# Attention in two levels of seven-product blocks: the last batch computes product 6 in whole blocks, and batch 6 puts its fourth pair of scores into product 2's banks

## The chip, the cores and the metric

The kernel runs on one core of one Trainium2 chip. The metric is device time in microseconds (us), the median of the runs. All data is 32-bit floating point. Engines by their short names: PE (TensorE, matrix products), PEld (its weight loads), DVE (VectorE), ACT (ScalarE), POOL (GpSimd) and SP (which only issues transfers).

## The reference

For each of 8 batches, with x of 512 x 1024 and a context x2 of 512 x 1024:

```python
q = einsum('bcn,dc->bnd', x1, Wq) + bq        # 1024 x 64
k = einsum('bcn,dc->bdn', x2, Wk) + bk[:, None]
v = einsum('bcn,dc->bdn', x2, Wv) + bv[:, None]
attn = softmax(einsum('bnd,bdm->bnm', q, k), axis=2)
out = einsum('bcm,bnm->bcn', v, attn) + x1     # 512 x 1024
```

## The kernel before

**The algebra.** Since each row of the attention sums to one, the values are applied last: with e the exponentials of the scores (m by n), y = x2 e, divided by the sums of e over m (the denominators), and out = Wv y + bv + x1. Both products, y and out ("o"), are done in 2 x 2 blocks by seven products instead of eight, as in Strassen's scheme in Winograd's form. The left blocks are called `a` (of x2) or `w` (of Wv), the right blocks `t` (of e) or `y`. `MULT` gives for each product its two operands, its PSUM banks and whether it opens them: 1 is 11 x 11 in banks a; 2 is 12 x 21 in c; 6 is S2 x T2, on a; 7 is S3 x T3, in c; 5 is S1 x T1, on a; 3 is S4 x 22, on a; 4 is 22 x T4, on c. S1 to S4 and T1 to T4 are sums of blocks, made by DVE, by ACT with accumulating transfers, or by transfers alone.

**Whole blocks and a second level.** A product of y can be done in whole blocks (`multiply`, L392: two halves of four matmuls of 128 x 128 by 128 x 512, L407, each half then copied out by ACT, L418), or by a second level of seven inner products of quarter size (L474: two matmuls of 256 columns each, recorded as four). The second level needs sums of its own, made on DVE: four left ones (`inner_left`, L447, 128 x 256 each) and three right ones (`inner_right`, L463 of 128 x 1024, L466 and L467 of 128 x 512). `multiply_seeded` (products 1, 2, 7 and 3) starts in fresh banks and ends with `complete` on DVE (L517). `multiply_joined` (5 and 6) leaves its parts in an SBUF tile d (ACT, L483), completes it (L551) and joins it with banks a (L566, two halves); after product 6, `reseed` (L573) copies the joined sums back into banks a. Their two extra accumulators, "chain" and "third", are taken from the pool `ps_s`, tag "sc", which has two buffers.

**Scores.** `scores_and(n, 0, i_bank, "c", ...)` computes the four pairs of scores of the next batch's first half (L240), each copied by ACT (L249). They use the same two "sc" buffers in turn, but the pair number `i_bank` uses banks c0 and c1 (two copies, L247). Then DVE takes the running maximum (`folds`, L260).

**Order.** The whole order is written out by hand under a manual schedule. `period(s, n, nn, nnn)` is one batch s with the next ones n, nn, nnn (None past the end); each engine executes its own instructions strictly in that order. `weave` interleaves lists of steps, one of each list in turn. The flag `six` says whether product 6 is done in the second level; before the change that holds for batches 2 to 5 and for batch 7, the last one. Batch 6 (where nn is None) does it in whole blocks, and so do 0 and 1.

**The last batch before the change**, in order: product 1; the sums of e for the second denominator (L260) with product 6's sums between them; `total` (L268 on DVE, then POOL's reduction across partitions, L288, and a small transfer, L290); product 2, with hooks on ACT that copy banks a (L361); y11 (L597); the first reciprocal (L296); `begin_s4` and `end_s4`; product 6, with hooks on ACT that copy the first operand of T4 (L349; POOL adds T2 by transfer, L350); the sums for 5 and for 7's left side; completion and joins of 6; reseed; T3 on DVE (L331); 7's right sums; S4's left sums for product 3; product 5, its completion, the second reciprocal, its joins woven with product 3's right sums; product 7 and y22; product 4's sums; product 3; the scaling of y (L588) and its sums (L375, L377); product 4; the scaling of y21; then the seven products of o (1, 6, 2, 5, 7, 4, 3; L427 and L407) and the output (L626, L636, L644, L648).

**S4** of a batch is begun by a load on SP's queue (L167) and finished by a transfer on POOL's queue that accumulates S2 onto it (L171). In the last batch SP's queue holds, ahead of that load, the last outputs of batch 6 (L664) and the four loads of x1 (L140) that the output adds.

Of the kernel before, what the change touches and what calls it, by code (L numbers as in the profile page):

```python
# [12 lines left out]
ALU = mybir.AluOpType  # L13
# [3 lines left out]
def kernel(  # L17
# [236 lines left out]
    def fold(s, h, i, kind, op):  # L254

        e = s.e[h]
        if i == 1:
            s.mx[h] = sb.tile([P, 2, H], F32, tag="fold", name=f"{kind}_{s.b}_{h}", bufs=2)
        f = s.mx[h]
        nc.vector.tensor_tensor(f, e[:, :, 0, :] if i == 1 else f, e[:, :, i, :], op)  # L260
# [9 lines left out]
    def folds(s, h, kind, op):  # L270

        return [lambda i=i: fold(s, h, i, kind, op) for i in range(1, MH)]

    def weave(*rows):

        for steps in zip_longest(*rows):
            for step in steps:
                if step:
                    step()
# [83 lines left out]
    def sums_e(s, *ks):  # L363
        parts = [{n: v[:, i : i + 2, :] for n, v in s.t.items()} for i in (0, 2)]
        return [lambda k=k, part=part: right_sums(part, k) for k in ks for part in parts]

    def sum_e(s, *ks):
        weave(sums_e(s, *ks))
# [70 lines left out]
    def inner_left(s, i, x, tag):  # L439

        v = {f"{p + 1}{q + 1}": x[:, ts(q, MH // 2), ts(p, P)] for p in range(2) for q in range(2)}
        sums = sb.tile([P, 4, MH // 2, P], F32, tag=tag, name=f"aI{i}_{s.b}")
        v |= {step[0]: sums[:, z] for z, step in enumerate(LEFT)}
        s.inner[i] = v

        def make(k, x, y, op):
            return lambda: nc.vector.tensor_tensor(v[k], v[x], v[y], op)  # L447

        return [make(*step) for step in LEFT]

    def inner_right(s, i, x, *tags):

        v = {
            f"{q + 1}{r + 1}": x[:, ts(q, MH // 2), ts(r, H // 2)] for q in range(2) for r in range(2)
        }
        last = 4 // len(tags)
        shape = [P, last, MH // 2, H // 2]
        sums = [sb.tile(shape, F32, tag=t, name=f"eI{i}{t}_{s.b}") for t in tags]
        both, t2, t4 = sums[0][:, 0:2], sums[-1][:, last - 2], sums[-1][:, last - 1]
        part = x.rearrange("p (q k) (r n) -> p q k r n", q=2, r=2)  # L460
        s.inner[i, "t"] = v | {"T1": both[:, 0], "T3": both[:, 1], "T2": t2, "T4": t4}
        return [
            lambda: nc.vector.tensor_tensor(  # L463
                both, part[:, :, :, 1, :], part[:, 0].rearrange("p k r n -> p r k n"), ALU.subtract
            ),
            lambda: nc.vector.tensor_tensor(t2, both[:, 0], v["22"], ALU.subtract),  # L466
            lambda: nc.vector.tensor_tensor(t4, v["21"], t2, ALU.add),  # L467
        ]
# [101 lines left out]
    def reseed(s):  # L570

        for j in range(2):
            nc.scalar.copy(s.bank["a", j], s.tmp[6][:, j, :])  # L573
# [27 lines left out]
    def evict_y(s, k):  # L601

        weave(evictions_y(s, k))
# [198 lines left out]
    def scores_and(n, h, i_bank, bank, project):  # L802

        for i in range(MH):
            scores(n, h, i, bank if i == i_bank else None)()
        return project()
# [4 lines left out]
    def period(s, n, nn, nnn):  # L811

        late = s.b >= 1
        six = late and (n is None or s.b >= 2 and nn is not None)

        def first(i):
            multiply(s, "y", i, s.a, s.t, MH)
# [17 lines left out]
                load_x(nnn, x1)  # L835

        def scores_0():
            then = scores_and(n, 0, 1, "c", next_queries if nn else nothing)
            if six:
                reseed(s)  # L840
            return then
# [11 lines left out]
        if s.b == 0:  # L853
            open_t(s)
            first(1)
            head_second(s, n)
            sum_e(s, "T1", "T2")
            total(s, 0)
            load_a(n, "11")
            first(2)  # L860
            evict_y(s, "11")
            keys(n)
            load_x(nn, x1)
            sum_t4(s)
            sums(s, 1)
            shares(s, 0)
            sum_e(s, "T3")
            load_a(n, "21", "22")
            first(6)
            scores_0()  # L870
            weave(folds(n, 0, "max", ALU.max))
            fold_halves(n, 0, ALU.max)
            highest(n, 0)
            weave(inner_left(s, 4, s.a["22"], "a12"), inner_right(s, 4, s.t["T4"], "eT2"))
            lefts_3 = inner_left(s, 3, s.a["S4"], "aI3")
            shares(s, 1)
            first(5)
            weave(lefts_3, inner_right(s, 3, s.t["22"], "eT1"))
            for i in range(MH):
                lower(n, 0, i)  # L880
            first(7)
            copy_7(s, 0)
            copy_7(s, 1)
            complete_3 = multiply_seeded(s, 3, "r")
            complete_3()
            evict_t3(s)
            evict_y(s, "22")
            scale_y(s, "T3", "11", "22")
        else:
            complete_1 = multiply_seeded(s, 1, "y11")  # L890
            adds = folds(s, 1, "sum", ALU.add)
            if six:
                weave(
                    adds,
                    [nothing, complete_1] + inner_right(s, 6, s.t["T2"], "yT1", "yT2"),
                    [nothing, nothing] + inner_left(s, 6, s.a["S2"], "i2"),
                )
            else:
                weave(adds, [nothing, complete_1] + inner_left(s, 7, s.a["S3"], "yT4"))
            total(s, 1)  # L900
            hooks = {5: lambda: copy_u1(s, 0), 4: lambda: copy_u1(s, 1)}
            if n:
                hooks |= {6: lambda: sum_t3(s, 0), 3: lambda: sum_t3(s, 2)}
            complete_2 = multiply_seeded(s, 2, "y22", hooks)
            complete_2()
            evict_y(s, "11")
            invert(s, 0)
            begin_s4(s)
            end_s4(s)
            sum_t4(s)  # L910
            evict_q = None
            if six:
                hooks = {6: lambda: copy_t4(s, 0), 5: lambda: copy_t4(s, 2)}
                complete_6, *join_6 = multiply_joined(s, 6, "v", hooks)
                lefts_5 = [] if n else inner_left(s, 5, s.a["S1"], "a11")
                weave(
                    inner_right(s, 5, s.t["T1"], "y21", "u1"), lefts_5, inner_left(s, 7, s.a["S3"], "yT4")
                )
                complete_6()
                weave(join_6)  # L920
                if n:
                    evict_q = scores_0()
                    weave(inner_left(s, 5, s.a["S1"], "i2"))
                    weave(folds(n, 0, "max", ALU.max))
                else:
                    reseed(s)
                    sum_e(s, "T3")
            else:
                copy_t4(s, 0)
                copy_t4(s, 2)  # L930
                first(6)
                weave(inner_right(s, 5, s.t["T1"], "y21", "u1"), inner_left(s, 5, s.a["S1"], "i2"))
                evict_q = scores_0()
                weave(folds(n, 0, "max", ALU.max))
            rights_7 = inner_right(s, 7, s.t["T3"], "yT1", "yT2")
            weave(rights_7, [nothing, nothing] + inner_left(s, 3, s.a["S4"], "aI3"))
            complete_5, *join_5 = multiply_joined(s, 5, "r", {6: evict_q} if nn else {})
            complete_5()
            if n:
                fold_halves(n, 0, ALU.max)  # L940
                highest(n, 0)
            spread(s, 0)
            shares(s, 1)
            weave(join_5, inner_right(s, 3, s.t["22"], "eT1"))
            if n:
                lower(n, 0, 0)
            complete_7 = multiply_seeded(s, 7, "y12")
            complete_7()
            evict_y(s, "22")
            if n:  # L950
                for i in range(1, MH):
                    lower(n, 0, i)
            else:
                weave(inner_left(s, 4, s.a["22"], "a12"), inner_right(s, 4, s.t["T4"], "eT2"))

            hooks = {2: lambda: copy_7(s, 0), 5: lambda: copy_7(s, 1)}
            if n:
                hooks |= {6: lambda: exponential(n, 0, 0), 4: lambda: exponential(n, 0, 1)}
            complete_3 = multiply_seeded(s, 3, "r", hooks)
            complete_3()  # L960
            evict_t3(s)
# [153 lines left out]
```

## Time and profile before

| what | us |
|---|---|
| median of 3 runs (lowest, highest) | 685.46 (685.11, 685.80) |
| the profiled execution's own time | 684.92 |
| its span | 683.1 |
| PE busy | 669.0 (98%) |
| DVE busy | 625.4 (92%) |
| ACT busy | 345.8 (51%) |
| POOL busy | 217.7 (32%) |

The span is the time between the first and the last instruction of the profiled execution; its own time, which the runs also measure, is 1.8 us longer. Times within the span are counted from its start. In the windows of the trace the last stages look so:

| stretch | us | PE busy | DVE busy | granted clock |
|---|---|---|---|---|
| 579.4 to 603.4: products of o, batch 6 | 24.00 | 24.00 | 23.76 | 1.00 |
| 603.4 to 615.4: products 1 and 2, batch 7 | 12.00 | 12.00 | 11.30 | 1.00 |
| 615.4 to 630.9: product 6 and the start of 5 | 15.50 | 8.42 | 15.47 | 1.00 |
| 630.9 to 655.2: the rest of 5, then 7, 3 and 4 | 24.30 | 24.30 | 21.65 | 0.93 |
| 655.2 to 683.1: products of o, output | 27.90 | 24.10 | 15.25 | 0.98 |

A busy time of PE is not PE at its peak, and the share over the whole span is an average over stages with different limits. The mean granted clock of the execution is 0.997.

### The profile page before, as it was taken

The numbers are of one execution on the slowest core, as the hardware profiler recorded it, in microseconds if no ns is written. First come the engines' busy times: TensorE is split into PE (matmuls) and PEld (weight loads), VectorE is DVE, ScalarE is ACT, GpSimd is POOL, SyncE is SP. The second block draws the span as 40 slices with busy tenths as digits, with TensorE's granted clock in tenths as the row PEclk, the third lists the DMA queues.
The fourth block names the chain that finished last, engine by engine and source line by source line (L and its number), as shares of the span: only waits on it lengthen the run. The fifth ranks groups of instructions, "written<-read, shape, count | busy, mean of one in ns | idle before, by whom it ended". The sixth has DMA issues, their size and how long they took to land.

```text
span 683.1 us, 7499 instructions
## 1 busy us (share of the span) xinstructions
PE 669.0 (98%) x2504; PEld 415.0 (61%) x2504; DVE 625.4 (92%) x826; ACT 345.8 (51%) x595; POOL 217.7 (32%) x189
## 2 busy tenths in 40 slices
PE   9999999999999999999999999999999999995997
PEld 5333554756558665668647685486755676474863
DVE  1999998989999999999999999999999889999884
ACT  2734266546455564473754656545645548443320
POOL 0124215341435314451144512434143621443100
PEclk9999999999999999999999999999999999999999
DMA  9666658997996969969699796998789784498503
GB/s 302 267 204 228 153 214 146 253 192 229 249 246 186 228 181 292 227 183 262 172 277 237 162 284 171 257 249 155 233 197 192 222 174 73 93 207 264 120 14 110
DMA packets 52790, 138.45 MB, mean 203 GB/s; under 512 B 5776, under 2 KB 8080, under 8 KB 52752
## 3 DMA queue, kind: packets, MB, share of 16 engines
q0 software_dynamic: 23472, 58.27, 47.3%
q1 hardware_dynamic: 28992, 79.31, 32.0%
q10 hardware_dynamic: 288, 0.39, 0.2%
q8 instruction: 20, 0.33, 0.2%
q14 instruction: 18, 0.15, 0.1%
HBM read 90.97 MB, written 16.81 MB: 158 GB/s over the span
## 4 chain that ended last, share of the span: by engine, by line
PE 93%; DVE 4%; DMA 1%; ACT 1%; issue 1%; SPq 0%; DVEq 0%; ACTq 0%
PE ps_oa L407 12%; PE ps_ya L474 10%; PE ps_oc L407 8%; PE ps_yc L474 8%; PE ps_s L240 6%; PE ps_ya L407 5%; PE ps_o L407 4%; PE ps_o L427 4%; PE ps_q L193 4%; PE ps_k L193 3%; PE ps_i4chain L474 3%; PE ps_i3chain L474 3%; PE ps_i5chain L474 3%; PE ps_i7chain L474 3%; PE ps_i1chain L474 3%; PE ps_i2chain L474 2%
## 5 line engine op out<-in xcount | busy, mean ns | idle before, releaser
L288 POOL PARTITION_ALL_REDUCE den<-half x16 | 51.6, 3225 | 91.2 <-DVE half L268 91.2
L283 POOL PARTITION_ALL_REDUCE top<-max x16 | 31.7, 1980 | 131.3 <-DVE few L296 58.2
L318 DVE TENSOR_TENSOR e<-e,top 128x1024 f32<-128x1024 f32 x60 | 69.8, 1213 | 0.0
L322 ACT ACTIVATE e<-e 128x1024 f32<-128x1024 f32 x60 | 61.8, 1057 | 6.2 <-DVE e L318 5.5
L407 PE MATMUL ps_oa<-yT,w_S 128*128 128x512 f32 x128 | 57.5, 592 | 0.0
L407 PE MATMUL ps_oc<-yT,w 128*128 128x512 f32 x128 | 57.4, 592 | 0.0
L667 POOL DMA_DIRECT2D sum<-e x21 | 28.9, 1377 | 84.3 <-ACT sum L672 36.1
L249 ACT COPY e<-ps_s 128x1024 f32<-128x1024 f32 x46 | 45.6, 1031 | 12.2 <-PE ps_s L240 7.2
L240 PE MATMUL ps_s<-q,k 64*128 64x512 f32 x188 | 47.8, 608 | 0.9 <-ACT q L693 0.8
L407 PEld LDWEIGHTS ps_oa<-yT,w_S 128*128 128x128 f32 x128 | 24.3, 190 | 30.6 <-issue 30.6
L407 PEld LDWEIGHTS ps_oc<-yT,w 128*128 128x128 f32 x128 | 24.3, 190 | 30.6 <-issue 29.9
L260 DVE TENSOR_TENSOR max<-max,e 128x1024 f32<-128x1024 f32 x30 | 36.7, 1222 | 2.2 <-DVE max L260 0.5
L418 ACT COPY uo<-ps_oa 128x512 f32<-128x512 f32 x32 | 18.7, 585 | 35.1 <-PE ps_oa L407 34.0
L240 PEld LDWEIGHTS ps_s<-q,k 64*128 64x128 f32 x188 | 17.0, 186 | 23.0 <-issue 16.3
L511 ACT COPY ps_ya<-ps_i1chain 128x256 f32<-128x256 f32 x28 | 10.0, 357 | 40.8 <-PE ps_i1chain L474 37.3
L588 DVE TENSOR_TENSOR y<-y,den 128x1024 f32<-128x1024 f32 x24 | 30.4, 1293 | 0.3
L407 PE MATMUL ps_oa<-y,w_S 128*128 128x512 f32 (+1 forms) x68 | 28.8, 567 | 0.0
L407 PE MATMUL ps_o<-y,w 128*128 128x512 f32 x64 | 28.8, 592 | 0.0
L427 PE MATMUL ps_o<-y,w 128*128 128x512 f32 x64 | 28.8, 592 | 0.0
L407 PE MATMUL ps_ya<-eT,aS 128*128 128x512 f32 x64 | 28.3, 595 | 0.0
L193 PE MATMUL ps_k<-x_in_x_dram,wqk_sb 128*64 128x512 f32 x112 | 26.0, 600 | 0.4 <-DMA x_in_x_dram<-in_x_dram 0.4
L331 DVE TENSOR_TENSOR eT<-eT,e 128x1024 f32<-128x1024 f32 x16 | 26.1, 1637 | 0.0
(217 smaller groups left out, 1655.1 us busy)
## 6 DMA issues: line engine op xcount, KB each, us to landing
x_in_x_dram<-in_x_dram SPq DMA_DIRECT2D x60, 512.0 KB, 8.4
a<-in_x2T_dram SPq DMA_DIRECT2D x32, 512.0 KB, 9.9
sum<-e POOLq DMA_DIRECT2D x21, 512.0 KB, 9.1
aS<-in_x2T_dram SPq DMA_DIRECT2D x14, 512.0 KB, 6.3
aS<-in_x2T_dram POOLq DMA_DIRECT2D x14, 512.0 KB, 7.6
uo<-in_x_dram POOLq DMA_DIRECT2D x14, 512.0 KB, 10.4
r<-in_x_dram POOLq DMA_DIRECT2D x14, 512.0 KB, 11.2
out_dram<-r SPq DMA_DIRECT2D x14, 512.0 KB, 4.6
```

The lines of the kernel that those rows point to most:

```text
L193: nc.tensor.matmul(ps[r, :], w_sb[:, c, :], s.x[:, c, ts(h, H)], start=(c == 0), stop=(c == CT - 1),)
L240: nc.tensor.matmul(ps[g], s.k[r, ts(i, P)], s.q[r, ts(h, H)], start=True, stop=True)
L249: nc.scalar.copy(e[:, :, i, :], whole)
L260: nc.vector.tensor_tensor(f, e[:, :, 0, :] if i == 1 else f, e[:, :, i, :], op)
L283: nc.gpsimd.partition_all_reduce(s.top[h], s.half[h], P, ReduceOp.max)
L288: nc.gpsimd.partition_all_reduce(s.den[h], s.half[h], P, ReduceOp.add)
L318: nc.vector.tensor_tensor(e, e, top, ALU.subtract)
L322: nc.scalar.activation(e, e, AF.Exp)
L407: nc.tensor.matmul(ps[:, n], left[ka][:, k, ts(j, P)], right[kb][:, k, n], start=opens and k == 0, stop=i in (2, 3, 4) and k == n_k - 1, s ...
L427: nc.tensor.matmul(ps, w["11"][:, k, ts(j, P)], s.y["11"][:, k, :], start=k == 0, stop=False, skip_group_check=True)
L474: nc.tensor.matmul(ps, s.inner[i][ka][:, k, :], s.inner[i, "t"][kb][:, k, :], start=opens and k == 0, stop=z in (2, 3, 4) and k == MH // 2 ...
L588: nc.vector.tensor_tensor(s.y[k], s.y[k], rden, ALU.mult)
```

## The change

Two things change in `period`. The flag `six` no longer holds for the last batch: its product 6 is done in whole blocks, so its inner sums, completion, joins and the reseeding copies are no longer there, and the copies of T4 stand before the product. Product 7's four left sums in the last batch move from beside product 5's sums to behind T3, beside 7's right sums. And in batch 6 (where nn is None) the pair of scores that uses banks c is number 3, the fourth, instead of number 1, the second.

```diff
-        six = late and (n is None or s.b >= 2 and nn is not None)
+        six = s.b >= 2 and nn is not None
...
-            then = scores_and(n, 0, 1, "c", next_queries if nn else nothing)
+            then = scores_and(n, 0, 1 if nn else 3, "c", next_queries if nn else nothing)
...
+            elif n:
+                weave(adds, [nothing, complete_1] + inner_left(s, 7, s.a["S3"], "yT4"))
             else:
-                weave(adds, [nothing, complete_1] + inner_left(s, 7, s.a["S3"], "yT4"))
+                weave(adds, [nothing, complete_1])
...
             if six:
                 hooks = {6: lambda: copy_t4(s, 0), 5: lambda: copy_t4(s, 2)}
                 complete_6, *join_6 = multiply_joined(s, 6, "v", hooks)
-                lefts_5 = [] if n else inner_left(s, 5, s.a["S1"], "a11")
                 weave(
-                    inner_right(s, 5, s.t["T1"], "y21", "u1"), lefts_5, inner_left(s, 7, s.a["S3"], "yT4")
+                    inner_right(s, 5, s.t["T1"], "y21", "u1"), [], inner_left(s, 7, s.a["S3"], "yT4")
                 )
                 complete_6()
                 weave(join_6)
-                if n:
-                    evict_q = scores_0()
-                    weave(inner_left(s, 5, s.a["S1"], "i2"))
-                    weave(folds(n, 0, "max", ALU.max))
-                else:
-                    reseed(s)
-                    sum_e(s, "T3")
+                evict_q = scores_0()
+                weave(inner_left(s, 5, s.a["S1"], "i2"))
+                weave(folds(n, 0, "max", ALU.max))
             else:
                 copy_t4(s, 0)
                 copy_t4(s, 2)
                 first(6)
                 weave(inner_right(s, 5, s.t["T1"], "y21", "u1"), inner_left(s, 5, s.a["S1"], "i2"))
-                evict_q = scores_0()
-                weave(folds(n, 0, "max", ALU.max))
+                if n:
+                    evict_q = scores_0()
+                    weave(folds(n, 0, "max", ALU.max))
+                else:
+                    sum_e(s, "T3")
             rights_7 = inner_right(s, 7, s.t["T3"], "yT1", "yT2")
+            if n is None:
+                weave(rights_7, inner_left(s, 7, s.a["S3"], "yT4"))
+                rights_7 = []
             weave(rights_7, [nothing, nothing] + inner_left(s, 3, s.a["S4"], "aI3"))
```

For batches 0 to 5 the instructions and their order are the same as before.

## The prediction

> **What bounds the kernel now.** I read the page first, then the chain of waits over the last two batches, then each engine's timeline there.
>
> ```profile
> span 683.1 us, 7499 instructions
> ...
> PE 93%; DVE 4%; DMA 1%; ACT 1%; issue 1%; SPq 0%; DVEq 0%; ACTq 0%
> ```
>
> TensorE (PE) carries 93% of the chain, so in most of the span work taken from another engine buys nothing. The last batch is the exception. The chain of waits shows VectorE (DVE) alone ending last from 608.69 to 629.3 (start us, length us, what):
>
> ```profile
> 613.36 1.23 DVE sum L260
> ...
> 616.32 1.14 DVE eI6yT L463
> ...
> 626.68 1.34 DVE aI L447 x4
> ...
> 628.63 0.61 DVE d L566
> ...
> 629.32 0.66 ACT ps_ya L573 x2
> ...
> 630.86 2.07 PE ps_i5chain L474 x4
> 632.93 1.60 PE ps_ya L474 x4
> ```
>
> The sums for product 6 (L463 to L467, L447), the sums for 5 and 7, the completion of 6 and its joins (L551, L566) and the two reseeding copies stand between PE and product 5. PE's timeline shows what they cost it there: idle 1.54 us before 617.93, 0.77 before 619.81 and 4.77 before 630.86, 7.1 us in all. Behind the last of them it also runs at half clock (the windows; the column after POOL is the granted clock):
>
> ```profile
> 628.00:630.90 2.90, 0.04 (x1) 0.04 (x1) 2.90 (x6) 1.58 (x4) 0.72 (x2) 1.00 0.24 89
> 630.90:632.00 1.10, 1.10 (x3) 0.92 (x4) 1.10 (x2) 0.18 (x1) 1.10 (x4) 0.50 0.44 82
> ...
> 635.00:636.00 1.00, 1.00 (x6) 0.88 (x5) 0.82 (x3) 0.57 (x2) 0.00 (x0) 1.00 1.14 221
> ```
>
> Two cold groups of four records there took 2.07 and 1.60 us where a warm one takes 0.86: 1.95 us more.
>
> The next limit is a transfer, not an engine. Product 3 of this batch needs S4, which is loaded on SP's queue behind the four loads of x1, and completed by an accumulating transfer from POOL's queue:
>
> ```profile
> 618.08 2.92 SPq L140 DMA_DIRECT2D x_in_x_dram<-in_x_dram  x4
> 621.12 0.55 SPq L167 DMA_DIRECT2D aS<-in_x2T_dram  x1
> ```
>
> ```profile
> 630.18 0.88 POOL L171 DMA_DIRECT2D aS<-aS  x1 [4.70 <-DMA aS<-in_x2T_dram]
> ```
>
> ```profile
> 635.15 0.76 DVE L447 TENSOR_TENSOR aI<-aS 128x256 f32<-128x256 f32 x2 [0.35 <-DMA aS<-aS]
> ...
> 642.73 0.70 DVE L517 TENSOR_TENSOR ps_yc<-ps_yc,v 128x512 f32<-128x512 f32 x1 [1.58 <-ACT ps_yc L511]
> ...
> 648.77 0.70 DVE L517 TENSOR_TENSOR ps_ya<-ps_ya,v 128x512 f32<-128x512 f32 x1 [0.48 <-ACT ps_ya L511]
> ...
> 659.86 1.22 DVE L588 TENSOR_TENSOR y<-y,den 128x1024 f32<-128x1024 f32 x1
> ```
>
> POOL waited 4.70 us for the load, and the accumulated S4 landed at 635.1: DVE's L447 at 635.15 is the first to read it and waited 0.35 us for it. The other three DVE rows are its waits after that (1.58 for product 7's copies, 0.48 for product 3's) and the scaling of y21, the last thing the third output product waits for.
>
> **The change, part by part.** All times are of this profiled execution: span 683.1, its own time 684.92, which is 0.54 below the median of the three timed runs, 685.46.
>
> Last batch, what goes from DVE. Four left and three right sums for product 6 lie between 616.23 and 620.04: 3.81 us. Completion and joins of 6 lie between 627.95 and 629.75: 1.80 us. Together 5.61 us; the two L573 copies (0.66 in the chain) go from ACT.
>
> What it adds on PE. Whole blocks are eight matmuls of 512 columns; batch 6 does the same and its chain piece "PE ps_ya L407 x16" is 6.87 us. The seven inner products are 7 x 0.86 = 6.04. So 0.83 us more PE work, but it waits for no sums: T2 is ready at 612.1, the copies of the bank at 615.8, so product 6 runs 615.37 to 622.24. On ACT two 0.58 us evictions of u6 replace six small copies.
>
> What moves. Product 7's four left sums (4 x 0.34 us) go from early DVE slots to behind T3 beside product 7's right sums: same work, no transfer of theirs. The copies of T4 on ACT come at about 615.8 instead of 621.21 and 623.20; their two transfers stay behind the S4 accumulation in POOL's queue, so T4 lands as before (by 641). POOL's reduction of the second denominator starts 3.81 us earlier; its small transfer and the row of the first denominator do too, but the second reciprocal stays behind S4 on DVE.
>
> DVE up to S4. The order becomes: sums, total, completion of 2, y11, then product 5's right sums at about 618.7 and its lefts by 622.8, T3 by 625.1, product 7's sums by about 629. Product 5 can start at 622.24, needs its first sums at 623.1 (ready 620.6), and ends at 628.3; product 7 follows from 628.3 to 634.3, its sums always ready first. So the three PE stalls (7.1) and the cold clock (1.95) go: 9.05 - 0.83 = 8.2 us by that. PE's product 7 ends at 634.3 where it ended at 643.17, 8.9 earlier (the rest are the waits of some tenths between them).
>
> What is late next: S4. DVE now reaches S4's left sums at 634.80 - 5.61 = 629.2 and waits there until 635.15; nothing in the change touches SP's queue, where S4 stands behind the x1 loads, and the accumulation is issued by POOL only when that load is in. Queued behind that wait on DVE are product 5's completion and joins, product 3's right sums, product 7's completion, y22 and product 4's sums. PE waits for it too, in product 3. So 5.6 of the 5.61 us saved turn into a wait, and from 635.15 on DVE runs as before, less the waits that a product 7 finished 8.9 us earlier takes away: 1.58 before 642.73 and 0.48 before 648.77. That is 2.06 us: y21's scaling ends at 661.08 - 2.06 = 659.02.
>
> PE after S4: product 3's first group 635.2 to 636.06, then a wait for its right sums (eI3, done 639.15), its end 644.9; product 4 to 650.9; two output products of 3.43 to 657.8; then it waits for y21 until 659.05. In the trace of before that third output product started at 661.96, with y21 ready 0.9 us earlier. Gain 661.96 - 659.05 = 2.9 us. From there to the end PE runs through, as before. Both denominators are in by then: the second one's spread is issued at 642.18 and took 3.4 us, needed at 648.6.
>
> Bounds on S4's landing, the one cost that the trace does not fix: if POOL issues quicker beside an idle DVE (L171 took 0.88, the quickest issue in these rows 0.54), 0.3 to 0.5 us better; if transfers collide otherwise, about 1 us worse. I take no change, since queue, source and neighbours are the same.
>
> The clock, a term to weigh. In the trace PE lost its clock after an idle 4.77 us, and not in 615.4 to 620.75, where it stood still 1.54 and 0.77 us. The change leaves 0.9 us idle before 635.2 and 3.1 before 639.15, with 0.86 of work between: between those two rows. Full clock costs 0; half clock 1.95 us on PE, against the 1.3 us that PE waits for y21: 0.65 net. I take 0, nearer to the interrupted idling.
>
> The Trainium skill ("TensorE: Matmul & The Clock Gate", What's actually happening) has the clock fall after one idle window of about 3.4 us; its closing table says to avoid gaps over about 3 us. By the first the 3.1 us gap is safe and the sum stays; by the second it is not and the gain is 2.25. The row of 0.50 after 4.77 us agrees with both, so no run here decides.
>
> Batch 6, the pair of scores in banks c moved from second to fourth. The timelines of ACT and then PE, before:
>
> ```profile
> 547.97 1.08 ACT L247 COPY e<-ps_sc 128x512 f32<-128x512 f32 x2
> 548.92 1.96 ACT L249 COPY e<-ps_s 128x1024 f32<-128x1024 f32 x2
> ```
>
> ```profile
> 550.02 1.13 PE L474 MATMUL ps_i5chain<-eT,aS 128*128 128x256 f32 x4 [0.50 <-ACT e L249]
> ```
>
> Product 5's two banks are freed by the copies of the last two scores in the ordinary banks. They were the third and fourth, so PE started at 550.02 and its second group waited until 551.15. Now they are the second and third: first group at about 549.9, second at 550.75, then a short wait for ACT, which copies the fourth pair first: product 5 ends about 0.4 us earlier on PE. But DVE decides here: its maxima start at 549.09 and run without a gap to 607.45, and the second score, now one copy instead of two, is there within 0.1 us of that. POOL's accumulations at 594 to 603, which feed SP's queue and so S4, come behind DVE's work too. I count 0; ends: 0.4 gained if PE's lead passes through, 0.1 lost if the third score's copy (ready at 550.3) makes DVE wait.
>
> Sum: 2.9 + 0. Span 680.2, profiled execution 682.0, median 685.46 - 2.9 = 682.6 us.
>
> **The rivals.** *S4 does not bind* (its landing follows the rest forward): PE keeps its 8.9 us and DVE follows, median about 676.6. For it: nothing but the size of the stall removed. Against it: 621.12 on SP, behind x1. Chance 0.06.
>
> *The clock falls* in product 3: gain 2.25, median 683.2. Chance 0.17.
>
> *Slower: S4's accumulation takes as long as elsewhere.* In the trace it lands 4.9 us after its issue in the last batch, and 8.6 to 9.5 us in the others that I looked up, where two more accumulations stand ahead of it in POOL's queue. Each us passes straight to DVE's end: +3.7 gives -2.9 + 3.7 = +0.8, median 686.3; +4.6 gives 687.2. It decides, that is, it makes the kernel slower, from about 4.3 us on. Against it: no transfer is put ahead of it. Chance 0.05.
>
> *No difference*: y21's chain is held by something else, such as the T4 transfers landing 2 us later, which then delay product 4's sums by what was won. T4 landed before 641.4 and is now needed at about 643.3 instead of 644.87: 1.9 us of margin. Chance 0.06.
>
> **How the numbers follow.** The forecast has 0.66. What a measurement of this kernel can tell from no change is about 0.2%, 1.4 us, so faster means under 684.1. Forecast, clock and free S4 are all faster: 0.89; no difference and part of the last rivals 0.07; slower 0.04. The range runs from 681.3 (S4 0.5 earlier, 0.4 from batch 6, and some of the free S4 case) to 684.0 (clock 0.65 and S4 0.8 later); outside it are most of the free S4 case and the two bad ones, under 0.2.
>
> **What would show it.** Right: PE's product 6 as L407 on ps_ya without a stall and product 5 and 7 behind it at clock 1.0; DVE idle about 6 us before L447 on aS, released by the transfer aS; about 3 us of PE wait for eI3; the third output product released by DVE's L588. Wrong: S4's L171 transfer landing at another place than 635 us, PE windows of 0.50 in product 3, an idle DVE before product 4's right sums, or DVE's first maximum in batch 6 more than 0.3 us away from 549.1.

## The result and the profile after

The changed kernel's median is 683.23 us (680.67 to 683.57, 9 runs), that of before 685.11 us in the runs beside it; the ratio is 0.9965, with an interval of 0.9954 to 0.9975. That is 2.4 us less (1.7 to 3.2). The profiled executions differ by 684.92 - 682.89 = 2.03 us, and this difference is explained below step by step. The page:

```profile
span 681.1 us, 7459 instructions
...
PE 84%; DMA 8%; DVE 2%; issue 2%; SPq 1%; ACT 1%; POOL 1%; DVEq 0%; POOLq 0%; ACTq 0%
```

DVE's share of the chain is down from 4% to 2%, and transfers, 1% before, are now 8%. Only 14.3 us of that, 2% of the span, are S4's two transfers. The rest lies far ahead, since the chain is now followed back by another way (22.5 us of the kernel's first loads, two accumulating transfers of 5.27 and 11.84 us that end before 608), and says nothing of the last batch. PE's timeline of the last batch (start us, length, engine, line, what, and idle time before it with its releaser):

```profile
615.63 7.03 PE L407 MATMUL ps_ya<-eT,aS 128*128 128x512 f32 x16
...
628.54 1.03 PE L474 MATMUL ps_i7chain<-e,a 128*128 128x256 f32 x4
...
635.86 1.13 PE L474 MATMUL ps_i3chain<-e,aS 128*128 128x256 f32 x4 [1.11 <-DMA aS<-aS]
640.06 1.53 PE L474 MATMUL ps_i3third<-eI3eT,aI 128*128 128x256 f32 x4 [3.07 <-DVE eI3eT L463]
...
659.92 3.60 PE L407 MATMUL ps_o<-y,w 128*128 128x512 f32 x8
```

Product 6 runs in 6.87 us of whole blocks without a wait, 5 follows it and 7 starts at 628.54, where before the change product 5's third group had waited until 630.86. Then PE waits 1.11 us for S4 and 3.07 us for DVE's sums, and its next groups are slow. DVE in the same stretch:

```profile
635.84 0.76 DVE L447 TENSOR_TENSOR aI<-aS 128x256 f32<-128x256 f32 x2 [6.71 <-DMA aS<-aS]
...
641.76 0.69 DVE L517 TENSOR_TENSOR ps_yc<-ps_yc,v 128x512 f32<-128x512 f32 x1
...
647.24 0.69 DVE L517 TENSOR_TENSOR ps_ya<-ps_ya,v 128x512 f32<-128x512 f32 x1
...
658.33 1.23 DVE L588 TENSOR_TENSOR y<-y,den 128x1024 f32<-128x1024 f32 x1
```

DVE waits 6.71 us for S4, where it had waited 0.35. Its former waits of 1.58 and 0.48 us (L517) are gone. Y21 is scaled at 659.56 (658.33 + 1.23), 0.4 us ahead of the product that needs it. The chain that ended last goes through the transfers (start us, length us, what):

```profile
620.94 9.37 DMA aS<-in_x2T_dram
...
630.89 4.92 DMA aS<-aS
...
640.06 1.53 PE ps_i3third L474 x4
641.59 1.71 PE ps_i3chain L474 x4
643.31 1.27 PE ps_ya L474 x4
```

Load of S4, accumulation of S4, then DVE, then PE: that is the order in which the last batch is now held. The windows show why the PE groups from 640.06 on are slow (the third number from the right is the granted clock):

```profile
640.00:641.00 1.00, 0.94 (x4) 0.79 (x4) 1.00 (x2) 0.00 (x0) 0.00 (x0) 0.80 0.92 209
641.00:642.00 1.00, 1.00 (x4) 0.68 (x3) 0.97 (x3) 0.32 (x1) 0.00 (x0) 0.50 0.36 137
...
644.00:645.00 1.00, 1.00 (x6) 0.90 (x5) 1.00 (x1) 0.20 (x1) 0.00 (x0) 1.00 0.61 172
```

### The profile page after: what moved, and what is told of

Read it like the earlier page. It is cut to its first block, busy times and chain, and to the rows that moved or that the text cites. A ratio compares the mean times of both kernels' runs of the same rounds, so it can differ in the third digit from the quotient of the medians.

```text
span 681.1 us, 7459 instructions
## 1 busy us (share of the span) xinstructions
PE 669.5 (98%) x2492; PEld 412.7 (61%) x2492; DVE 620.0 (91%) x816; ACT 344.4 (51%) x590; POOL 218.7 (32%) x189
## 4 chain that ended last, share of the span: by engine, by line
PE 84%; DMA 8%; DVE 2%; issue 2%; SPq 1%; ACT 1%; POOL 1%; DVEq 0%; POOLq 0%; ACTq 0%
PE ps_oa L407 11%; PE ps_ya L474 9%; PE ps_yc L474 7%; PE ps_oc L407 7%; PE ps_s L240 6%; PE ps_ya L407 5%; PE ps_q L193 4%; PE ps_o L407 4%; PE ps_o L427 4%; PE ps_k L193 3%; PE ps_i3chain L474 3%; PE ps_i4chain L474 3%; DMA sum<-e 3%; PE ps_i5chain L474 2%; PE ps_i1chain L474 2%; PE ps_i7chain L474 2%
## 5 line engine op out<-in xcount | busy, mean ns | idle before, releaser
L407 PE MATMUL ps_ya<-eT,aS 128*128 128x512 f32 x80 | 35.4, 595 | 0.0
L588 DVE TENSOR_TENSOR y<-y,den 128x1024 f32<-128x1024 f32 x24 | 30.4, 1294 | 0.3
L303 POOL DMA_DIRECT2D den<-row x16 | 10.0, 624 | 51.3 <-DMA row<-few 51.3
```

The costliest lines, as they stand in the source:

```text
L407: nc.tensor.matmul(ps[:, n], left[ka][:, k, ts(j, P)], right[kb][:, k, n], start=opens and k == 0, stop=i in (2, 3, 4) and k == n_k - 1, s ...
L588: nc.vector.tensor_tensor(s.y[k], s.y[k], rden, ALU.mult)
```

## The experiments

Two theories stand against each other. Mine: all is won in the last batch; S4's landing decides, and from its first reading on DVE, with some tenths from PE's clock. Against it: the moved pair of scores has a share; or S4's wait is incidental, and the scaling of y21 or PE's own work holds the end. Every ratio is to the kernel before, timed beside the kernel in question.

**Only the last batch, and only the pair.** The first kernel changes only the last batch and keeps batch 6's pair in second place; the second is the kernel before with only the pair moved to fourth place. The first against the changed kernel:

```diff
-            then = scores_and(n, 0, 1 if nn else 3, "c", next_queries if nn else nothing)
+            then = scores_and(n, 0, 1, "c", next_queries if nn else nothing)
```

> Only the last batch is changed; batch 6 keeps its second pair of scores in product 2's banks. My theory (all of the gain is made in the last batch, and is bound by the landing of S4): the same as the changed kernel within 0.3 us, that is 0.9965 of before, about 2 us less. Rival (the moved pair gives or takes a part): 0.4 us or more away from the changed kernel, and batch 6's first maximum on DVE shifted by that much against product 6's end.

> Only the pair of scores is moved, from second to fourth; the last batch is as before. My theory: within 0.2 us of before, since PE's second group of product 5 starts at the same time (it waited for ACT before, and now starts behind a pair that itself waited for ACT) and DVE's maxima start within 0.1 us. Rival (the pair matters by itself): 0.4 us faster, or slower if the third score's copy holds DVE up.

The last batch alone: 683.41 us, ratio 0.9972 (0.9961 to 0.9982). The pair alone: 685.00 us, ratio 0.9994 (0.9985 to 1.0003). The last batch makes the gain, and the pair makes none that can be told. PE's timeline of the changed kernel shows why the pair is nothing even on PE:

```profile
548.44 1.13 PE L240 MATMUL ps_s<-q,k 64*128 64x512 f32 x4 [0.32 <-ACT e L249]
...
551.32 1.03 PE L474 MATMUL ps_i5third<-eI5y,aI 128*128 128x256 f32 x4
```

The third pair now waits 0.32 us for ACT's copy of the first, and the pair in banks c comes behind it. From the first scores to product 5's second group it takes 551.32 - 546.12 = 5.20 us; before it was 550.99 - 545.82 = 5.17. One wait was exchanged for another.

**S4's load first.** In the changed kernel, the four loads of x1 are issued behind S4's load:

```diff
-        if n is None:
-            load_x(s, x1)
...
             begin_s4(s)
             end_s4(s)
+            if n is None:
+                load_x(s, x1)
             sum_t4(s)
```

> The changed kernel with the four loads of x1 of the last batch issued behind S4's load on SP's queue instead of ahead of it. My theory (S4's landing holds DVE and PE): S4's load is issued at about 618 instead of 620.9 and meets less traffic, S4 is whole at about 628 instead of 635.8, DVE's wait of 6.71 us and PE's waits of 1.11 and 3.07 us go, the clock stays at 1.00, and the third output product starts at about 653.5 instead of 659.9: 6.4 us less than the changed kernel, 8.4 less than before (0.988). Rival (S4's wait is incidental, and the scaling of y21 or PE's own work holds the end): less than 1 us.

Measured: 679.72 us, ratio 0.9922 (0.9910 to 0.9935), by the two ratios 3 us less than the changed kernel: S4 does bind, and the rival falls. But 6.4 us were expected. The chain of this kernel and DVE's first reading of S4:

```profile
618.63 5.89 DMA aS<-in_x2T_dram
...
625.11 8.49 DMA aS<-aS
```

```profile
633.62 0.76 DVE L447 TENSOR_TENSOR aI<-aS 128x256 f32<-128x256 f32 x2 [3.81 <-DMA aS<-aS]
```

The load is 2.3 us earlier and takes 5.89 us instead of 9.37, but the accumulation takes 8.49 us instead of 4.92, so S4 is there only at 633.6. DVE still waits 3.81 us for it. PE then waits for DVE twice:

```profile
637.85 1.10 PE L474 MATMUL ps_i3third<-eI3eT,aI 128*128 128x256 f32 x4 [1.71 <-DVE eI3eT L463]
...
657.39 3.70 PE L407 MATMUL ps_o<-y,w 128*128 128x512 f32 x8 [0.88 <-DVE y L588]
```

Its wait for the right sums is 1.71 us, its clock stays at 1.00, and at the third output product it is y21's scaling (L588) that it waits for, 0.88 us.

**The same exchange in the kernel before.**

> The kernel before with the same exchange on SP's queue: S4's load ahead of the four loads of x1. My theory: there only DVE's 0.35 us hangs on S4, so 0 to 0.4 us less than before. Rival (the order of these transfers matters by itself, for example through what the x1 loads do to others): 1 us or more, as in the changed kernel.

Measured: 685.54 us, ratio 1.0003 (0.9995 to 1.0012). DVE's wait for S4 is gone from its trace (L447 at 634.50), PE still idles 4.77 us ahead of product 5's third group at 630.64, and nothing that can be told is won: where product 6's sums and joins hold PE, the order of the loads is worth nothing.

**S4's load first, with the pair back in second place.**

> The changed kernel with S4's load first, and batch 6's pair of scores back in second place. My theory: the same as with S4 first alone (within 0.3 us): the pair moves neither PE's nor DVE's times in batch 6. Rival (what the pair gives was hidden behind S4 and shows once S4 no longer binds): slower by 0.4 us.

Measured: 678.97 us, ratio 0.9919 (0.9905 to 0.9932), which can't be told from the 0.9922 with the pair in fourth place. No gain of the pair shows once S4 is earlier.

**Product 7's left sums in their former place.**

```diff
-                weave(inner_right(s, 5, s.t["T1"], "y21", "u1"), inner_left(s, 5, s.a["S1"], "i2"))
+                lefts_7 = [] if n else inner_left(s, 7, s.a["S3"], "yT4")
+                weave(inner_right(s, 5, s.t["T1"], "y21", "u1"), inner_left(s, 5, s.a["S1"], "i2"), lefts_7)
...
-                weave(rights_7, inner_left(s, 7, s.a["S3"], "yT4"))
+                weave(rights_7)
```

> The changed kernel with product 7's four left sums in their former place, beside product 5's sums instead of behind T3. My theory: DVE has 6.7 us to spare before S4, so no difference from the changed kernel (within 0.2 us). Rival (the place of these sums is a part of the gain): slower by up to 1.4 us, their own time on DVE, with PE waiting for T3's sums before product 7.

Measured: 683.13 us, ratio 0.9969 (0.9959 to 0.9980), the same as the changed kernel. DVE waits 7.27 us for S4 here. The place of the four sums is no part of the gain while that wait stands behind them.

**PE kept at work.** In product 3 of the last batch, eight matmuls write a bank that nothing reads:

```diff
+            if s.b == B - 1 and i == 3 and z == 1:
+                keep_warm(s, 7, 2)
             inner_product(s, i, z, ps, opens)
+            if s.b == B - 1 and i == 3 and z == 1:
+                keep_warm(s, 3, 6)
...
+    def keep_warm(s, i, count):
+        for _ in range(count):
+            nc.tensor.matmul(
+                s.spare, s.inner[i]["11"][:, 0, :], s.inner[i, "t"]["11"][:, 0, :], start=True, stop=True
+            )
```

> The changed kernel with eight matmuls that nothing reads, into an unused bank, put into the last batch's product 3: two ahead of its first group, six behind it (3.4 us of PE at full clock, in the 4.2 us that PE waits). My theory (half clock in product 3 comes from this waiting, and costs 1.9 us on PE of which y21's scaling would take back all but about 0.3): the granted clock stays 1.00 through product 3, PE reaches the third output product at about 658.0, waits there for y21, and starts it at about 659.6: 0.3 us less than the changed kernel. Rival A (the clock's loss passes wholly to the end): 1.9 us less. Rival B (the clock does not follow PE's idling): 0.50 stays in product 3 and the time is the same.

```profile
637.18 2.75 PE L496 MATMUL ps_i3chain<-e,aS 128*128 128x256 f32 x12
640.42 1.10 PE L474 MATMUL ps_i3third<-eI3eT,aI 128*128 128x256 f32 x4 [0.48 <-ACT ps_ya L524]
...
659.96 3.70 PE L407 MATMUL ps_o<-y,w 128*128 128x512 f32 x8 [0.88 <-DVE y L601]
```

(L496 are the added matmuls; L496, L524 and L601 are counted in this kernel, whose lines are shifted.) The granted clock is 1.00 through the whole of product 3, so the half clock does come from PE's waiting: rival B falls. PE is then early and waits 0.88 us for y21. From DVE's first reading of S4 to the third output product it takes 659.96 - 636.19 = 23.77 us, and 659.92 - 635.84 = 24.08 in the changed kernel: 0.31 us, as expected, and not the 1.9 of rival A. The time of the runs, 682.95 us, ratio 0.9969 (0.9956 to 0.9981), is too blunt to show 0.3 us.

**x1 out of S4's way.** SP no longer loads x1; ACT issues the four loads behind its copies of product 7:

```diff
-        if n is None:
-            load_x(s, x1)
...
             complete_7 = multiply_seeded(s, 7, "y12")
+            if n is None:
+                load_x(s, x1, nc.scalar)
             complete_7()
```

> The changed kernel with the last batch's four loads of x1 issued by ACT behind its copies of product 7, instead of by SP ahead of S4's load. With S4 first, S4's accumulation took 8.49 us and not 4.92, and S4 still bound, at 633.6. My theory now (the accumulation is slowed by the x1 loads that run beside it): with nothing beside it S4 is loaded by about 623.5 and whole by about 628.5, DVE's wait for it goes (under 0.5 us), PE no longer waits in product 3, the third output product starts at about 654 and the time is 3 us less than with S4 first, about 676.5. Rival (the accumulation takes 8 to 9 us whenever S4's load is early, whatever runs beside it, as in the other batches): S4 at about 632, a DVE wait of 3 us, and a time within 1 us of S4 first (679).

> The kernel before with the same late loads of x1. My theory: S4 was not what held it, so within 0.4 us of before; product 6's sums and joins on DVE still hold product 5, with PE idle for about 7 us and half a clock behind it. Rival (the x1 loads' traffic slows other things in the last batch): 1 us or more less.

In the changed kernel: 676.56 us, ratio 0.9879 (0.9866 to 0.9893). The transfers of S4, with the time from issue to landing at the end of the line:

```profile
aS<-in_x2T_dram SPq DMA_DIRECT2D x1, 512.0 KB, 5.4
aS<-aS POOLq DMA_DIRECT2D x1, 512.0 KB, 5.0
```

With the x1 loads out of the way the accumulation takes 5.0 us, so it was they that stretched it to 8.49. By how much they stretch it differs: 8.10 us with the pair back in second place, but 6.1 in the kernel before with S4's load first, where it takes 4.8 with x1 late. Why it differs was not tried. In the kernel before, x1 late gives 685.25 us, ratio 1.0001 (0.9991 to 1.0011); there the same loads cost nothing that can be told. DVE's timeline of the changed kernel with x1 late, PE's, and its chain:

```profile
629.71 0.76 DVE L447 TENSOR_TENSOR aI<-aS 128x256 f32<-128x256 f32 x2
...
644.24 1.23 DVE L588 TENSOR_TENSOR yT<-yT,den 128x1024 f32<-128x1024 f32 x1 [1.26 <-DMA den<-row]
```

```profile
654.70 3.70 PE L407 MATMUL ps_o<-y,w 128*128 128x512 f32 x8 [0.49 <-DVE y L588]
```

```profile
637.61 6.54 DMA den<-row
```

L447 reads S4 without a wait. What is late next is the spread of the second denominator, 6.54 us beside the x1 loads. It holds DVE for 1.26 us and, through y21, PE for 0.49.

**x1 later still**, behind the copies of product 3:

> As with x1 loaded late by ACT, but behind the copies of product 3 instead of product 7. With x1 behind product 7, the spread of the second denominator took 6.54 us beside those loads, held DVE for 1.26 us and PE for 0.49 us. My theory: the spread takes about 3.4 us again, DVE's wait goes, PE runs through from product 6 to the end, and the third output product starts at about 654.0 instead of 654.7: 0.5 to 0.7 us less, about 676.0. Rival (x1 now comes too late for the output's first addition, which needs it 9 us before the end of the third output product): slower by 1 us or more.

Measured: 676.14 us, ratio 0.9871 (0.9850 to 0.9891). The spread takes 3.5 us again. The four loads, issued from 639.16 on, take 3.3 to 7.0 us, and the first addition of the output that reads x1 starts at 654.68, so the rival falls. On PE's timeline no wait is left from product 6 to the end:

```profile
633.70 1.03 PE L474 MATMUL ps_i3chain<-e,aS 128*128 128x256 f32 x4
...
652.76 3.60 PE L407 MATMUL ps_o<-y,w 128*128 128x512 f32 x8
```

From product 3's first group to the third output product it takes 652.76 - 633.70 = 19.06 us, in the kernel with x1 behind product 7 654.70 - 635.00 = 19.70: 0.64 us less, as expected. The ratios of the two kernels overlap, so the timed runs alone don't tell them apart. This is the fastest version, 0.0129 x 685.5 = 8.8 us under before, and its interval lies well below the changed kernel's.

One row over all runs carries the theory: the time from DVE's first reading of S4 to the third output product. It is 23.77 us in every kernel whose clock stayed up and whose S4 came late (633.62 to 657.39, 632.12 to 655.89, 636.19 to 659.96), and 24.08, 24.52 and 24.56 in the three profiled executions where the clock fell (the changed kernel, the last batch alone, product 7's sums early). Before, it was 661.96 - 635.15 = 26.81.

## Why the prediction was right

The forecast was 2.9 us; the profiled executions show 2.0 and the ratio 2.4. The mechanism came as forecast, the saved DVE time turning into a wait for S4. Three of the signs named in advance went the other way: S4 landed at 635.8 and not at 635, the clock was at 0.50 in product 3, and the third output product was not released by y21's scaling. The two misses behind them add up to 0.9 us, which the stated range had room for.

- *DVE's 5.61 us and the wait they turn into.* Right. DVE came to S4's left sums at 629.1 (forecast 629.2), and the saving became a wait there.
- *PE's product 6, 5 and 7 without a stall, 6.87 us for 6.* Right: 615.63 to 622.50, and product 7 from 628.54.
- *S4 at 635.15, unchanged.* Mis-sized by 0.69 us: 635.84. The load was issued 0.18 us earlier, but took 9.37 us instead of 8.5 and was in at 630.31 (620.94 + 9.37), and POOL issued the accumulation at 630.89 instead of 630.18. The accumulation itself took 4.92, as before. The longer load is no accident of one execution: it took 9.2 to 9.9 us in the three other kernels with this last batch and this order of loads. Why was not tried; the bounds given, 0.5 better to 1 worse, held it.
- *2.06 us of DVE waits gone behind S4.* Right within 0.2: from L447 to the end of y21's scaling it was 661.08 - 635.15 = 25.93 and is 659.56 - 635.84 = 23.72, 2.21 less.
- *The clock.* Taken as full, with 0.17 for the other case. The other case came: 0.50 from 640.59 to 644.00, and three groups of 1.53, 1.71 and 1.27 us in the chain instead of 0.86 each, 1.9 us on PE as the row of before had it. Net of y21 it cost 0.31 us in this execution (0.75 and 0.79 in the two other profiled ones where the clock fell), against the 0.65 that was priced. The step that failed is the choice between the two rows, not the price: it was made by the length of the waits, in one execution of the kernel before. The pair alone shows how little that row held: its last batch is that of before, and its clock fell already in product 6, behind waits of 1.60 and 0.77 us. What the clock followed is PE's busy time in stretches of 3.41 us (the last section), and in the stretch from 637.18 to 640.59 that was 0.53 us.
- *Batch 6 as nothing.* Right in sum and wrong in one step: PE's 0.4 us lead in product 5 was not there. The pair in banks c cannot start before the third pair, which waits 0.32 us for ACT. From there PE's groups start 0.95 to 0.97 us apart (548.44, 549.40, 550.35, 551.32), where the forecast had 0.85 between product 5's two.

So the gap of profile and forecast, 0.9 us, is 0.69 of S4's landing and 0.3 of the clock, less 0.15 from DVE. This is a comparison of two single executions, which differ by 0.3 us already at batch 6's first scores (545.82 and 546.12), ahead of anything changed. The rivals: a free S4 did not happen by itself. With x1 out of the way it came close to its price: 8.9 us were priced, and the ratio 0.9879 is 8.3. That 676.6 was forecast and 676.56 measured is in part luck, since the second denominator's spread and y21 still held that kernel. The slow accumulation, put at 8.6 us elsewhere, came in the experiment that let x1 run beside it, 8.49, not in the changed kernel.

## What to carry to other kernels

When work is taken off an engine that runs in a fixed order, look for the next instruction in that order that waits for a transfer: what is saved ahead of it can be no more than the time to that transfer's landing, and all that is queued behind it moves with it. Then ask whether that transfer has to be late: here four loads, needed some 25 us after S4, stood ahead of it and ran beside it, and moving them was worth 6.4 us (ratio 0.9965 to 0.9871), but only in the kernel whose sums had been taken away; in the kernel before, moving them behind product 7 was worth nothing that can be told.

## What the runs showed of the hardware

- The same accumulating transfer of 512 KB within SBUF took 4.92 us behind the x1 loads, 4.8 to 5.1 with nothing of theirs beside it, and 8.49, 8.10 and 6.1 in the three kernels where the x1 loads (2 MB from HBM, issued 3 to 7 us ahead of it) were still landing. The spread of one row over 128 partitions took 3.3 to 3.8 us where the x1 loads were not beside it and 6.54 beside them. Both are issued by POOL.
- The granted clock changed only at the ends of stretches of 3.41 us, which follow one another from the start and lie elsewhere in each execution: with nearly the same work on PE it fell at 640.59 in the changed kernel, at 638.37 in the last batch alone and at 637.51 with product 7's sums early. Half clock in the last two batches lasted one stretch (3.41 us) or two (6.83). In all twelve traces the full clock fell behind a stretch in which PE was busy for at most 1.49 us, and stayed behind one with at least 1.71:

| kernel | stretch (us) | PE busy in it | clock behind it |
|---|---|---|---|
| before | 627.47 to 630.88 | 0.02 | half |
| changed | 637.18 to 640.59 | 0.53 | half |
| the pair alone | 616.26 to 619.67 | 1.19 | half |
| the last batch alone | 634.95 to 638.37 | 1.49 | half |
| S4's load first | 634.47 to 637.88 | 1.71 | full |
| before, S4's load first | 615.12 to 618.54 | 1.85 | full |
| before | 617.23 to 620.64 | 1.94 | full |

- So the longest wait does not decide, and the same work can keep its clock in one execution and lose it in another: product 6 of before, with waits of 1.54 and 0.77 us, kept it, and the pair alone, with 1.60 and 0.77, lost it. The Trainium skill ("TensorE: Matmul & The Clock Gate", What's actually happening) speaks of an idle window of about 3.4 us; no single wait in the changed kernel was that long. Its closing table advises against idle gaps over about 3 us; the measurement is stricter, since gaps of 1.60 and 0.77 us in one stretch were enough. With matmuls in the waits of product 3 the clock stayed at 1.00.
- Where PE was still waiting in the first stretch of half clock (busy 0.91 to 2.45 us of 3.41 in five traces), a second followed; behind a stretch with at least 3.26 us of work the full clock was back. Both lengths came in the changed kernel too: of its nine executions five have a mean granted clock of 0.997, which one stretch of half clock makes of a span of 681 us, and four have 0.995, which two make. Their medians are 682.89 and 683.46 us.
